# Cross-attention with LayerNorm on one core: the residual and LayerNorm passes of six late tiles moved to PSUM, GpSimd's gain and shift passes separated, and every engine's order of work replaced

## The chip, the cores and the metric

The kernel runs on one core of one Trainium2 chip. The metric is the device time of one execution in microseconds (us). Five engines work at the same time, each through its own queue in program order: TensorE (PE, with its weight loads PEld), VectorE (DVE), ScalarE (ACT), GpSimd (POOL) and SyncE (SP), which only issues DMAs here. An engine waits for another one by a semaphore. SBUF is the on-chip memory, and PSUM holds the results of matmuls in eight banks of 128 x 512 float32.

## The reference

Four batches of 2048 rows attend to 77 context rows each, with 16 heads of width 32. The keys past a batch's length are masked out. The residual is the query itself, and a LayerNorm with gain and shift closes the layer.

```python
qs = (q @ wq).reshape(Bq, Lq, H, HD).transpose(0, 2, 1, 3)
ks_ = (k @ wk).reshape(Bq, Lk, H, HD).transpose(0, 2, 1, 3)
vs = (v @ wv).reshape(Bq, Lk, H, HD).transpose(0, 2, 1, 3)
scores = jnp.einsum('bhqd,bhkd->bhqk', qs, ks_) / jnp.sqrt(jnp.float32(HD))
scores = jnp.where(mask[:, None, :, :], -jnp.inf, scores)
attn_w = jax.nn.softmax(scores, axis=-1)
attn = jnp.einsum('bhqk,bhkd->bhqd', attn_w, vs)
attn = attn.transpose(0, 2, 1, 3).reshape(Bq, Lq, H * HD)
out = attn @ wo + q
mu = jnp.mean(out, axis=-1, keepdims=True)
var = jnp.mean((out - mu) ** 2, axis=-1, keepdims=True)
return (out - mu) / jnp.sqrt(var + EPS) * gamma + beta
```

x has shape (4, 2048, 512), the context (4, 77, 512), and every weight is 512 x 512, all float32.

## The kernel before

The 8192 rows are cut into 64 tiles of 128 rows, into 32 blocks of two tiles, and into 16 groups of four tiles. Products that must keep float32 accuracy are made from a high and a low part of each operand (names ending in h and l): three matmuls for each of four chunks of 128 input columns, so twelve matmuls of 128x512 for a projection. A tile passes through these steps; the letter is the word for the step in the list `ORDER`, and the lines are those of the profile of the kernel before.

- **Q, q** (L274, L288): TensorE projects the queries of a group into a PSUM bank, VectorE copies them out. The split operands come from **i** (ScalarE, L264) and **j** (GpSimd, L268).
- **S** (L398): the scores of a tile, 32 small matmuls into four banks, one for each head of a group of four.
- **T** (L415): VectorE adds the mask, finds the negative row maximum `nm` of a head, and moves the scores into one of three buffers `pbuf`.
- **e** (L430): ScalarE takes the exponentials in place, with the row sums.
- **r, n** (L440, L445): reciprocals on VectorE, then GpSimd multiplies a whole tile by them. For tile 63 these stand in halves (**h, m**, L451, L457).
- **t** (L466): VectorE transposes 32x32 blocks into `B`. **P** and **U** (L477) are the DMAs that regroup `B` into `PT`, twelve for a block, or for one of the tiles 62 and 63; the last letter of the word is the queue (s: SP, a: ACT, g: GpSimd).
- **V** (L491), or **W** for one tile (L506): the product with the values, into two banks. **a, b** or **c, d** (L520, L524): ScalarE rounds the result to its high part `AH`, VectorE forms the low part `AL` and so frees the bank.
- **x** (L532) loads the residual rows. **O** (L547): the output projection, twelve matmuls into a bank. **+** (L556): VectorE adds the residual, writes the sum into SBUF and frees the bank.
- **s** (L567, L568): mean and variance. For the tiles 0 to 55, **v** (L573 to L576) makes the scale and bias of two tiles on GpSimd, **k** (L582) applies them on ScalarE, and **f** (L586, L587) multiplies by `gam` and adds `bet` on GpSimd, two passes one behind the other.
- The tiles 56 to 63 go another way: **s** (L595, L597), **u** (L601, L602) on GpSimd for the inverse deviation, **y** (L613) on VectorE, which subtracts the mean and multiplies by `gam`, and **z** (L616) on VectorE, which multiplies by the inverse deviation and adds `bet`. For 62 and 63, **X** (L536) adds the residual on TensorE, so that no + is needed, and y reads PSUM. The rows of 56 to 59 lie in a buffer that the trace calls `xth`, those of 60 to 63 in `xtl`.
- **w** (L590): SP stores the tile.

Nothing is scheduled by a planner at build time. `ORDER` lists all words once, and the program is recorded in that order, so the sequence of an engine's own words in the list is the sequence of its queue. `SLOTS` says beside it which of an operand's buffers, or which PSUM bank ("mm"), each new tile takes. A word whose buffer still has a reader waits for that reader. The numbers behind a word are tile, block or group and a part: `T61.2` is the third quarter of the maxima of tile 61.

Of the kernel before, what the change touches and what calls it, by code (L numbers as in the profile page):

```python
# [13 lines left out]
ALU = mybir.AluOpType  # L14
# [40 lines left out]
M16.4 e7.1 T7.3 r6 T7.0 P1.8s P1.5s P1.11s P1.9s P1.1s e7.3 e5.1 P1.10s j6 x3 T5.2 q11 e5.2 T5.3 Q10 q10 Q13 q13 T7.2
e7.2 e7.0 Q12 n6 t6 e5.3 r7 n7 S9 T9.2 e9.2 q12 r5 n5 T9.3 Z1.s V0 Y0 Z3.s g9 g8 T9.0 t7 P3.7s P3.5s P3.2s P3.4s V1
a1.0 b1.0 i9 P3.3s P3.10s T9.1 a0.1 b0.1 a1.1 a0.0 t5 P2.0s Q14 b1.1 Z10.s P3.1s P2.6s S8 T8.3 e9.1 e9.3 P3.9s P3.0s
b0.0 T8.1 P3.8s O2 T8.0 i8 j8 j9 +2 s2 O3 T8.2 +3 e8.3 s3 S10 T10.1 v1 e9.0 r9 n9 P3.11s e8.0 M20.4 P3.6s P2.7s g10
T10.2 T10.0 e8.2 e8.1 r8 n8 e10.0 P2.1s O0 +0 q14 s0 t9 Z5.s k3 P2.11s Q15 T10.3 P2.9s f3 t8 k2 f2 e10.2 S11 T11.0
# [5 lines left out]
P5.5s S15 x5 P5.1s T15.3 T15.2 V4 P5.4s a4.0 b4.0 e14.3 T15.0 j11 e14.1 a4.1 e15.2 s4 b4.1 +5 r14 s5 v2 e15.3 e15.0
n14 Q17 Z4.s O9 P5.2s P5.9s P5.0s x8 P5.11s +9 T15.1 q17 P5.10s e15.1 k5 O8 +8 P6.4s S16 T16.0 T16.3 T16.2 e16.2 V5
a5.0 k4 P6.7s P6.2s t14 P6.6s P6.10s P6.0s P6.9s S17 T17.0 g12 P6.3s T17.3 T16.1 e16.1 e17.3 r15 b5.0 Q20 f0 s8 w0
P6.8s x12 P6.5s T17.1 s9 T17.2 a5.1 e16.3 b5.1 f5 n15 t15 v4 f4 P6.1s w5 P6.11s Q21 Q22 S18 T18.2 T18.1 e16.0 r16 g13
P7.6s e17.0 n16 k9 P7.9s P7.4s q20 q21 P7.2s T18.3 T18.0 e17.2 e17.1 r17 n17 P7.8s P7.11s x10 O11 V6 a6.0 b6.0 t16
P7.10s w4 S19 T19.0 +11 s11 t17 k8 f8 a6.1 i12 e18.0 i13 P7.7s f9 O10 w7 P7.0s P7.1s j13 T19.3 b6.1 e18.3 e18.2 T19.1  # L70
q22 Q23 q23 k6 e19.0 e18.1 T19.2 e19.2 r18 O12 +12 S20 T20.1 e20.1 T20.2 e20.2 P8.7s j12 +10 s10 P8.2s P7.5s P7.3s O13
x13 +13 s13 T20.3 P8.0s T20.0 n18 t18 P8.3s g15 P8.10s e19.1 i15 e19.3 r19 Q25 q25 f6 v5 k11 S21 T21.2 P8.5s w9 P8.8s
P8.11s V7 P8.1s a7.0 b7.0 w8 T21.3 x14 P8.6s e20.3 Q24 T21.0 a7.1 b7.1 n19 s12 j15 t19 T21.1 e21.3 e20.0 r20 P8.4s
e21.2 w6 g14 P8.9s x15 P9.5s P9.4s S22 T22.1 T22.0 T22.3 T22.2 M24.4 P9.9s x17 O14 O15 +15 x16 e21.0 k10 e21.1 r21
P9.6s P9.3s v6 f11 i14 +14 n20 t20 V8 a8.1 a8.0 b8.0 n21 t21 S23 T23.1 T23.3 k12 f12 f10 j14 e22.3 b8.1 s14 q24 e22.1
e23.1 T23.2 e23.3 Q27 q27 Q26 P9.1s P9.0s q26 T23.0 s15 e23.2 e22.2 P9.2s P9.7s g16 P10.0s O16 +16 P10.1s P9.11s P9.8s
P9.10s O17 e22.0 r22 +17 P10.10s S24 T24.0 T24.3 T24.2 P10.4s P10.2s P10.6s T24.1 w11 i16 e23.0 k13 r23 w10 n22 t22
e24.3 V9 a9.0 P10.7s P10.8s x19 S25 b9.0 T25.1 s16 v7 e24.0 g17 x18 L2 a9.1 b9.1 P10.5s T25.2 T25.3 k15 w12 P10.11s
j16 P10.3s P10.9s n23 f13 w13 s17 v8 T25.0 Q28 t23 P11.5s P11.6s g18 Q29 e25.1 e24.2 e24.1 r24 n24 q28 O18 +18 S26
P11.2s T26.1 T26.0 P11.11s x20 P11.10s q29 T26.2 T26.3 s18 i17 e25.3 k17 e25.0 f17 e25.2 r25 w17 P11.8s O19 +19 s19  # L80
P11.1s t24 M32.4 P11.4s P11.0s n25 P11.7s t25 V10 S27 T27.1 T27.3 e26.2 k14 e26.0 a10.1 e26.3 a10.0 b10.0 e26.1 f15
r26 P12.7s b10.1 j17 v9 T27.0 Q30 q30 k16 e27.3 P12.5s Q31 q31 T27.2 x21 P12.1s P11.9s O21 P11.3s P12.8s x23 S28 T28.0
T28.2 T28.1 +21 e27.0 k19 O20 n26 t26 s21 e27.1 e27.2 i18 V11 a11.0 b11.0 M44.4 e28.2 S29 T28.3 a11.1 r27 b11.1 O22
O23 T29.2 T29.1 +20 s20 P12.6s T29.0 w15 f14 f19 f16 n27 e28.1 t27 P12.9s S30 T29.3 T30.2 P12.3s P12.0s P12.11s g19
e28.3 e28.0 P12.2s r28 M40.4 x22 w19 +22 +23 Q35 q35 P12.4s i19 j19 Q32 e29.0 T30.0 T30.1 e29.1 e29.2 e29.3 r29 x24
P12.10s P13.4s P13.11s P13.9s P13.5s P13.8s P13.1s P13.6s w14 w16 g20 n28 t28 v10 P13.3s k20 s23 S31 T31.0 n29 s22
T30.3 V12 e30.1 a12.0 k18 e30.0 f18 j18 v11 T31.3 e31.3 t29 e30.2 a12.1 P13.0s P13.7s e30.3 x25 w18 P14.3s P13.2s
P13.10s T31.1 e31.0 e31.1 b12.0 P14.5s P14.7s T31.2 f20 b12.1 Q34 q34 Q33 e31.2 r30 n30 q32 k23 i20 O25 x27 g21 x26
P14.9s +25 q33 s25 P14.1s O24 +24 r31 n31 f23 P14.4s P14.6s S32 T32.3 T32.2 e32.3 e32.2 P14.0s P14.2s P14.8s P14.11s
P14.10s V13 a13.0 S33 a13.1 T32.0 e32.0 t30 s24 v12 T33.0 T33.3 e33.3 Q38 t31 P15.10s j20 T32.1 e32.1 e33.0 T33.1  # L90
e33.1 b13.0 q38 r32 n32 k24 f24 Q37 P15.5s P15.1s k21 P15.8s f21 b13.1 T33.2 Q36 q36 i21 k25 S34 T34.1 T34.0 T34.2 g23
T34.3 t32 V14 a14.1 P15.0s P15.4s P15.3s P15.11s b14.1 a14.0 M36.4 P15.9s e33.2 r33 n33 O26 b14.0 +26 S35 T35.3 T35.2
P15.7s w23 w21 P15.6s w20 x29 e34.3 j21 e34.2 k22 f22 T35.1 e34.1 e34.0 t33 P15.2s Q39 P16.10s P16.0s P16.1s P16.2s
i23 q39 T35.0 O27 q37 +27 g22 s26 s27 v13 w22 P16.4s L3 O29 +29 e35.3 r34 S36 T36.2 T36.1 T36.0 e35.2 e35.0 P16.7s x28
P16.3s P16.11s e36.1 e35.1 x32 T36.3 P16.6s n34 t34 S37 T37.3 r35 T37.1 P16.8s T37.2 e36.2 Q42 f25 Q41 q41 V15 q42 S38
n35 P16.9s t35 P16.5s P17.4s j23 P17.5s P17.1s T38.0 P17.0s i22 j22 k27 x30 P17.11s T38.2 f27 e36.3 e36.0 T37.0 r36
# [76 lines left out]
def xattn_layernorm(  # L173
# [384 lines left out]
    def hold(t):  # L558
        nc.scalar.copy(once(tmps, t // 2, [P, 2, D], F32, "xtf")[:, t % 2], pos.pop(t))
# [199 lines left out]
```

## Time and profile before

| what | us |
|---|---|
| median of 3 runs | 522.41 (521.73 to 524.83) |
| the profiled execution, its own time | 522.61 |
| its span, first to last instruction | 520.8 |
| busy in that span: DVE | 473.8 |
| busy in that span: ACT | 465.6 |
| busy in that span: POOL | 427.3 |

The profile is one execution. "Busy" is the time in which an engine has at least one instruction under way; matmuls overlap by design, so a busy TensorE may still have short pauses between groups. The view by windows gives busy times for stretches of the span. The chain of waits follows the work that ended last back from the end: each step goes to what released it. The word "issue" there means that the engine waited for nothing that the profile shows. The granted clock is the share of TensorE's full clock.

### The profile page before, as it was taken

Reading aid. Unit: us, or ns where it says so; the run is one execution under the profiler, and the core shown is the slowest. Engines: PE = TensorE matmul, PEld = TensorE weight load, DVE = VectorE, ACT = ScalarE, POOL = GpSimd, SP = SyncE. Lnnn points to the kernel's source line nnn. Section 1 sums busy time; section 2 is a strip of 40 time slices with the busy share of each in tenths; the row PEclk is TensorE's granted clock in tenths of the full one; section 3 lists DMA queues with packets and bytes.
Section 4 is the critical chain, followed back from the end, with each engine's and each line's share of the span. In section 5 each row is a group of like instructions: output and inputs, shape, how many; then the busy total and the mean of one; then the engine's idle time right before and its main releaser. Section 6 shows DMA issues by size and latency. Waiting matters only on the chain.

```text
span 520.8 us, 20280 instructions
## 1 busy us (share of the span) xinstructions
PE 502.8 (97%) x6833; PEld 385.6 (74%) x6833; DVE 473.8 (91%) x2562; ACT 465.6 (89%) x2223; POOL 427.3 (82%) x387
## 2 busy tenths in 40 slices
PE   8999999999999999999999999999999999989983
PEld 6987767777777677777778777777777777767752
DVE  5798989999988999999899899999998999879997
ACT  6699999899899999999999999999999999979430
POOL 2574737857888889988988989989888998978896
PEclk9999999999999999999999999999999999989998
DMA  8946776877768786779878679967768777876635
GB/s 302 402 132 206 176 212 180 236 185 187 195 183 260 210 227 213 216 219 240 202 214 228 176 226 276 230 178 200 203 183 256 224 204 199 251 218 161 184 98 222
DMA packets 59261, 110.85 MB, mean 213 GB/s; under 512 B 9430, under 2 KB 11758, under 8 KB 59158
## 3 DMA queue, kind: packets, MB, share of 16 engines
q1 hardware_dynamic: 55702, 102.75, 69.4%
q0 software_dynamic: 2496, 5.77, 4.0%
q8 instruction: 54, 0.88, 0.8%
q10 hardware_dynamic: 960, 1.05, 0.7%
q14 instruction: 49, 0.40, 0.3%
HBM read 41.79 MB, written 16.78 MB: 112 GB/s over the span
## 4 chain that ended last, share of the span: by engine, by line
PE 69%; DVE 13%; DMA 6%; POOL 5%; SPq 3%; issue 2%; ACT 1%; ACTq 0%; DVEq 0%; POOLq 0%
PE po L547 25%; PE pq L274 25%; PE pa L491 9%; PE sc L398 8%; DVE pbuf L415 2%; DVE B L466 2%; SPq L477 2%; DMA PT<-B 2%; PE pk L297 1%; POOL pbuf L445 1%; POOL o L587 1%; POOL o L586 1%; DMA xtf<-xT 1%; DVE st L595 1%; ACT pbuf L430 1%
## 5 line engine op out<-in xcount | busy, mean ns | idle before, releaser
L430 ACT ACTIVATE pbuf<-pbuf,nm 128x77 f32<-128x77 f32 x1024 | 352.7, 353 | 8.7 <-DVE nm L415 8.4
L430 ACT ACTIVATION_READ_ACCUMULATOR pbuf<-pbuf,nm 128x1 f32 x1024 | 198.0, 193 | 0.0
L445 POOL TENSOR_TENSOR pbuf<-pbuf,ri 128x1232 f32<-128x1232 f32 x63 | 142.7, 2269 | 43.4 <-DVE ri L440 33.5
L415 DVE CUSTOM_DVE_ANT_0 pbuf<-sc,mb 128x77 f32<-128x77 f32 x1024 | 171.1, 231 | 6.5 <-PE sc L398 4.1
L547 PE MATMUL po<-woh,AH 128*128 128x512 f32 x256 | 104.1, 407 | 0.2 <-PE sc L398 0.2
L547 PE MATMUL po<-woh,AL 128*128 128x512 f32 x256 | 100.8, 394 | 3.0 <-DVE AL L524 3.0
L274 PE MATMUL pq<-xth,wqh 128*128 128x512 f32 (+1 forms) x256 | 100.8, 394 | 1.0 <-DVE nm L415 0.5
L547 PE MATMUL po<-wol,AH 128*128 128x512 f32 x256 | 100.5, 392 | 0.0
L466 DVE STREAM_TRANSPOSE B<-pbuf 128x1280 f32<-128x1280 f32 x64 | 95.8, 1500 | 3.0 <-POOL pbuf L445 1.3
L274 PE MATMUL pq<-xtl,wqh 128*128 128x512 f32 (+1 forms) x256 | 98.2, 383 | 0.0
L274 PE MATMUL pq<-xth,wql 128*128 128x512 f32 (+1 forms) x256 | 98.1, 383 | 0.0
L415 DVE DVE_READ_ACCUMULATOR2_ANT nm<- 128x1 f32 x1024 | 84.2, 82 | 0.0
L587 POOL TENSOR_TENSOR o<-o,bet 128x512 f32<-128x512 f32 x56 | 73.2, 1307 | 4.4
L586 POOL TENSOR_TENSOR o<-o,gam 128x512 f32<-128x512 f32 x56 | 73.1, 1305 | 3.3 <-ACT o L582 3.3
L268 POOL TENSOR_TENSOR xtl<-xtf,xth 128x1024 fp32r<-128x1024 f32 x28 | 67.6, 2418 | 7.8 <-ACT xth L264 7.8
L398 PEld LDWEIGHTS sc<-kct,q 32*64 32x64 f32 x4096 | 51.9, 130 | 24.8 <-issue 17.7
L398 PE MATMUL sc<-kct,q 32*64 32x77 f32 x4096 | 61.6, 238 | 3.0 <-issue 2.3
L491 PE MATMUL pa<-PT,vsb 96*32 96x256 f32 x992 | 59.7, 382 | 0.9 <-DMA vsb<-v 0.9
L547 PEld LDWEIGHTS po<-woh,AL 128*128 128x128 f32 x256 | 48.4, 189 | 15.0 <-DVE AL L524 4.7
L274 PEld LDWEIGHTS pq<-xth,wqh 128*128 128x128 f32 x256 | 48.0, 188 | 15.2 <-issue 2.5
L547 PEld LDWEIGHTS po<-woh,AH 128*128 128x128 f32 x256 | 48.3, 189 | 13.8 <-issue 1.6
L547 PEld LDWEIGHTS po<-wol,AH 128*128 128x128 f32 x256 | 48.5, 190 | 9.8 <-issue 0.5
(99 smaller groups left out, 647.0 us busy)
## 6 DMA issues: line engine op xcount, KB each, us to landing
PT<-B SPq DMA_DIRECT2D x343, 128.0 KB, 3.4
xtf<-xT SPq DMA_DIRECT2D x28, 512.0 KB, 5.0
o<-x SPq DMA_DIRECT2D x56, 256.0 KB, 5.3
out<-o SPq DMA_DIRECT2D x56, 256.0 KB, 4.2
PT<-B POOLq DMA_DIRECT2D x25, 128.0 KB, 4.4
xtf<-xT SPq DMA_DIRECT2D x4, 256.0 KB
stage_a<-wq SPq DMA_DIRECT2D x4, 256.0 KB, 5.0
stage_a<-wk SPq DMA_DIRECT2D x4, 256.0 KB
```

The source lines that it names most:

```text
L268: nc.gpsimd.tensor_tensor(l[:, c : c + 2], fx.pop((g, c)), xh[g][:, c : c + 2].bitcast(F32), ALU.subtract)
L274: nc.tensor.matmul(pq, w[:, c, m * P : (m + 1) * P], r[g][:, c, rs], start=(n == 0), stop=(n == 11))
L398: mm = nc.tensor.matmul(sc[j][r0 : r0 + SR, g * NK : (g + 1) * NK], qs[q, g, rs.start + r0 : rs.start + r0 + SR], kct[q, g, t // TPB, keys ...
L415: nc.vector.tensor_tensor_reduce(pb[:, h // 2, (h % 2) * NK : (h % 2 + 1) * NK], scs[t][j][:, g * NK : (g + 1) * NK], mb[:, t % TPB, keys_ ...
L430: nc.scalar.activation(pb[:, h // 2, (h % 2) * NK : (h % 2 + 1) * NK], pb[:, h // 2, (h % 2) * NK : (h % 2 + 1) * NK], AF.Exp, bias=nmax[t ...
L445: nc.gpsimd.tensor_tensor(pv, pv, rv.to_broadcast((P, NP, 2, NK)), ALU.mult)
L466: nc.vector.transpose(bt.rearrange("p c q r -> p q c r"), pbuf[t % NPB].rearrange("p q (c r) -> p q c r", c=5),)
L477: parts.setdefault(b, []).append(queue.dma_start(pt[32 * c : 32 * c + 32, i, :, cols], src))
L491: nc.tensor.matmul(pas[b, g // 2][HD * j : HD * (j + 1), (g % 2) * BLK : (g % 2 + 1) * BLK], vsb[:, 2 * b // TPB, h % 2, HD * (h // 2) : H ...
L547: nc.tensor.matmul(pos[t], a[:, c, rs], w[:, c, :], start=(first and c == 0 and n == 0), stop=(c == NC_D - 1 and n == 2),)
L586: nc.gpsimd.tensor_tensor(o, o, gam, ALU.mult)
L587: nc.gpsimd.tensor_tensor(o, o, bet, ALU.add)
```

## The change

The diff does three things.

1. A new word `&` (`residual_psum`) takes the place of `+` for the tiles 56 to 61. It adds the residual in place in the PSUM bank. The statistics of these tiles then read PSUM, `centre` works in place in PSUM, and `finish` reads PSUM and writes the SBUF tile that is stored. The bank is free only after `finish`. For 62 and 63 the residual stays on TensorE, and `centre` now leaves its result in PSUM too.
2. `affine` (word `f`) is split into `gain` (word `f`, the multiplication by `gam`) and `shift` (a new word `)`, the addition of `bet`), so that other GpSimd work can stand between the two passes of a tile.
3. `ORDER` and `SLOTS` are replaced. Apart from the six `&` and the 56 `)`, the new list has the same words as the old one, DMA queues included.

```diff
+    def residual_psum(t):
+        nc.vector.tensor_tensor(pos[t], pos[t], od[t], ALU.add)
+
...
-    def affine(t):
-        o = od[t]
-        nc.gpsimd.tensor_tensor(o, o, gam, ALU.mult)
-        nc.gpsimd.tensor_tensor(o, o, bet, ALU.add)
+    def gain(t):
+        nc.gpsimd.tensor_tensor(od[t], od[t], gam, ALU.mult)
+
+    def shift(t):
+        nc.gpsimd.tensor_tensor(od[t], od[t], bet, ALU.add)
...
     def centre(t):
-        nc.vector.scalar_tensor_tensor(od[t], pos.pop(t, od[t]), mvs[t, 1][:, 0:1], gam, ALU.subtract, ALU.mult)
+        v = pos.get(t, od[t])
+        nc.vector.scalar_tensor_tensor(v, v, mvs[t, 1][:, 0:1], gam, ALU.subtract, ALU.mult)
 
     def finish(t):
-        nc.vector.scalar_tensor_tensor(od[t], od[t], mvs[t, 1][:, 2:3], bet, ALU.mult, ALU.add)
+        nc.vector.scalar_tensor_tensor(od[t], pos.pop(t, od[t]), mvs[t, 1][:, 2:3], bet, ALU.mult, ALU.add)
...
-62.3a U62.0a U62.4a W62 U63.1a y59 u58 v27 k55 k47 f53 U63.2s U63.11s W63 w53 y58 z57 w57 k54 f54 w54 +60 s60 z56 u60
...
+b30.0 U63.8g f53 y56 z56 a30.1 b30.1 U62.11a U63.2s U63.10g U63.1a f55 f52 s58 u58 y59 X62 O61 &61 z59 s61 u61 z57 O60
...
-    "o": "765401234567321706507316240576143206751234601720315642073612534",
+    "o": "765401234567143650247153064261370562140765231407523460745216025",
```

The lists below are the rows of an engine's queue, each with its line, its operation, what it writes and what it reads; the first number in a name is the tile or block, and the last one, or the only one, is a running number. The lines of the new kernel lie a few numbers higher: L557 is `+`, L560 is `&`, L619 `centre`, L622 `finish`, L589 `gain`, L592 `shift`.

**VectorE in the last microseconds.** This is the stretch around the low parts of block 30 (AL_30), before:

```order
L524 TENSOR_TENSOR AL_30_8914<-pa_30_0_8890,AH_30_8908 128x512
L613 SCALAR_TENSOR_TENSOR xth_14_7678<-xth_14_7678,mvt_57_8872,gam_76 128x512
L524 TENSOR_TENSOR AL_30_8914<-pa_30_1_8891,AH_30_8908 128x512
L613 SCALAR_TENSOR_TENSOR xth_14_7678<-xth_14_7678,mvt_59_8886,gam_76 128x512
L613 SCALAR_TENSOR_TENSOR xth_14_7678<-xth_14_7678,mvt_58_8912,gam_76 128x512
L616 SCALAR_TENSOR_TENSOR xth_14_7678<-xth_14_7678,mvt_57_8872,bet_77 128x512
L556 TENSOR_TENSOR xtl_15_7768<-po_60_8921,xtl_15_7768 128x512
L595 BN_STATS st_60_9009<-xtl_15_7768 128x6
L597 BN_AGGR mvt_60_9011<-st_60_9009 128x2
L616 SCALAR_TENSOR_TENSOR xth_14_7678<-xth_14_7678,mvt_56_8804,bet_77 128x512
```

And the same stretch in the new kernel:

```order
L525 TENSOR_TENSOR AL_30_8917<-pa_30_0_8896,AH_30_8914 128x512
L619 SCALAR_TENSOR_TENSOR po_56_8834<-po_56_8834,mvt_56_8857,gam_76 128x512
L622 SCALAR_TENSOR_TENSOR xth_14_7670<-po_56_8834,mvt_56_8857,bet_77 128x512
L525 TENSOR_TENSOR AL_30_8917<-pa_30_1_8897,AH_30_8914 128x512
L600 BN_STATS st_58_8931<-po_58_8874 128x6
L602 BN_AGGR mvt_58_8933<-st_58_8931 128x2
L619 SCALAR_TENSOR_TENSOR po_59_8861<-po_59_8861,mvt_59_8891,gam_76 128x512
L560 TENSOR_TENSOR po_61_8940<-po_61_8940,xtl_15_7695 128x512
L622 SCALAR_TENSOR_TENSOR xth_14_7670<-po_59_8861,mvt_59_8891,bet_77 128x512
L600 BN_STATS st_61_8955<-po_61_8940 128x6
```

The residuals, statistics, centrings and finishes now have a PSUM operand (`po`) where they had only SBUF ones (`xth`, `xtl`), and the finish of tile 56 stands ahead of the second low part of block 30 instead of behind the statistics of tile 60.

**TensorE around the scores of the tiles 60 and 61.** Before, the product of block 27 stands between the two (x8: eight such rows in a row):

```order
L398 MATMUL sc_60_1_8259<-kct_74,q_15_8049 64x77
L398 MATMUL sc_60_2_8260<-kct_74,q_15_8049 64x77
L398 MATMUL sc_60_3_8261<-kct_74,q_15_8049 64x77
L491 MATMUL pa_27_0_8308<-PT_27_7975,vsb_75 32x256 x8
L491 MATMUL pa_27_1_8309<-PT_27_7975,vsb_75 32x256 x8
L398 MATMUL sc_61_0_8350<-kct_74,q_15_8049 64x77
```

In the new kernel the output projection of tile 50 follows the scores of tile 60:

```order
L399 MATMUL sc_60_1_8268<-kct_74,q_15_7997 64x77
L399 MATMUL sc_60_2_8269<-kct_74,q_15_7997 64x77
L399 MATMUL sc_60_3_8270<-kct_74,q_15_7997 64x77
L548 MATMUL po_50_8339<-woh_72,AH_25_7960 128x512
L548 MATMUL po_50_8339<-wol_73,AH_25_7960 128x512
L548 MATMUL po_50_8339<-woh_72,AL_25_7982 128x512
```

The twelve matmuls of that projection now lie between the scores of 60 and 61, and the product of block 27 comes after the scores of 61.

**GpSimd between the normalisations of the tiles 62 and 63.** Before:

```order
L445 TENSOR_TENSOR pbuf2_82<-pbuf2_82,ri_62_8699 128x8x154
L477 DMA PT_30_8664<-B_30_8584 32x2x512
L586 TENSOR_TENSOR o_51_8068<-o_51_8068,gam_76 128x512
L587 TENSOR_TENSOR o_51_8068<-o_51_8068,bet_77 128x512
L573 TENSOR_TENSOR rn_26_8770<-mv_26_8729,small_78 128x2
L574 TENSOR_TENSOR rn_26_8770<-rn_26_8770,small_78 128x2
L575 TENSOR_TENSOR rn_26_8770<-mv_26_8729,rn_26_8770 128x2
L576 TENSOR_TENSOR rn_26_8770<-rn_26_8770,small_78 128x2
L477 DMA PT_31_8757<-B_31_8755 32x2x256
L457 TENSOR_TENSOR pbuf0_80<-pbuf0_80,ri_63_8792 128x4x154 x2
```

And in the new kernel:

```order
L446 TENSOR_TENSOR pbuf2_82<-pbuf2_82,ri_62_8681 128x8x154
L589 TENSOR_TENSOR o_51_8068<-o_51_8068,gam_76 128x512
L592 TENSOR_TENSOR o_50_7588<-o_50_7588,bet_77 128x512
L592 TENSOR_TENSOR o_51_8068<-o_51_8068,bet_77 128x512
L458 TENSOR_TENSOR pbuf0_80<-pbuf0_80,ri_63_8782 128x4x154 x2
```

The four small steps of block 26 and a DMA have moved behind the normalisation of tile 63, and the shift of tile 50, now apart from its gain, stands in their place.

More of the change, by code (lines that the diff above doesn't have):

```diff
@@ L55 @@
[L55 to L59, printed above, removed]
@@ L65 @@
[L65 to L69, printed above, removed]
@@ L70 @@
[L70 to L94, printed above, removed]
@@ L154 @@
     "xtl": "10101010101010101",
[L155 to L156 removed]
+    "xtf": "010101100110101001100101010110",
+    "PT": "10100101010101010101010101010101010",
     "B": "0101011010101010101010101010101010",
```

165 lines of the change are left out of this document (99 added, 66 removed).

## The prediction

> **What bounds the kernel now.** I read the page's busy times first, then the windows, to see where TensorE is not busy, then the chain of waits at those places.
>
> ```profile
> PE 502.8 (97%) x6833; PEld 385.6 (74%) x6833; DVE 473.8 (91%) x2562; ACT 465.6 (89%) x2223; POOL 427.3 (82%) x387
> ...
> core 0: us, PE busy (x) PEld busy (x) DVE busy (x) ACT busy (x) POOL busy (x), PEclk, DMA share, GB/s
> 0.00:52.00 52.00, 49.96 (x632) 41.64 (x633) 40.24 (x215) 42.37 (x183) 25.77 (x27) 1.00 0.77 261
> 52.00:416.00 364.00, 360.77 (x5060) 276.16 (x5059) 339.76 (x1934) 351.86 (x1700) 310.73 (x257) 1.00 0.77 212
> 416.00:442.00 26.00, 26.00 (x431) 18.94 (x429) 25.34 (x169) 26.00 (x141) 23.86 (x24) 1.00 0.72 204
> 442.00:468.00 26.00, 23.91 (x364) 18.65 (x360) 20.85 (x115) 22.11 (x112) 22.29 (x25) 0.93 0.84 233
> 468.00:494.00 26.00, 26.00 (x248) 19.04 (x233) 24.56 (x100) 18.67 (x88) 22.92 (x29) 1.00 0.67 176
> 494.00:507.00 13.00, 11.08 (x118) 7.65 (x111) 12.83 (x20) 4.57 (x7) 12.36 (x18) 1.00 0.35 108
> 507.00:521.00 14.00, 5.12 (x22) 3.55 (x20) 10.25 (x16) 0.00 (x0) 9.39 (x13) 0.82 0.53 206
> ```
>
> TensorE carries the kernel: from 52 to 416 us it lacks 364.00 - 360.77 = 3.2 us. A new order with the same matmuls can give back those 3.2 us, 2.1 us between 442 and 468, and what the end costs. In the last 27 us it is no longer TensorE: from 494 to 507 VectorE is busy 12.83 of 13 us, and it runs on after TensorE is done. So the time is a TensorE stream of some 490 us and a VectorE tail.
>
> The one large pause in the stream, in the chain of waits:
>
> ```profile
> 454.00 0.88 PE sc L398 x52
> 454.88 1.86 PE pa L491 x32
> 456.75 0.81 PE sc L398 x49
> 457.56 2.08 issue
> 459.65 0.36 PE sc L398 x6
> 460.01 7.31 PE po L547 x24
> ...
> 468.20 5.64 PE po L547 x24
> ```
>
> TensorE stops for 2.08 us within the scores of tile 61, for nothing that the profile shows as a wait. The two projections behind it (24 matmuls) then take 7.31 us, where the next two take 5.64: 1.67 us more. The windows there give the clock, and the DMA view of 456 to 459 us a packet:
>
> ```profile
> 460.00:465.00 5.00, 5.00 (x17) 3.94 (x16) 2.93 (x27) 1.91 (x9) 3.90 (x5) 0.66 0.56 161
> 465.00:468.00 3.00, 3.00 (x75) 2.31 (x73) 1.97 (x12) 3.00 (x19) 1.43 (x1) 1.00 0.92 269
> ...
> q8 instruction: 54, 0.88, 0.8%
> ...
> q8 instruction: 1, 0.02, 2.5%
> ```
>
> The granted clock was 0.66 in the 5 us behind the pause, and 1.00 later. The whole run has 54 packets on the instruction queue q8 (first q8 row), one of them in just these 3 us (second). TensorE has 2 x 6833 = 13,666 records, 253 for each packet. From the scores of tile 60 to those of 61 it goes through 128 + 64 + 128 = 320 records in 3.6 us (454.00 to 457.56), more than a packet's worth. I read the pause as instructions that came too late.
>
> **The change part by part.**
>
> *The PSUM passes.* No instruction is added on VectorE; operands change. What they cost now:
>
> ```profile
> L616 DVE SCALAR_TENSOR_TENSOR xth<-xth,mvt,bet x4: 747/1266/1760, 499.5 to 504.1; 128x512 f32<-128x512 f32 x4
> L616 DVE SCALAR_TENSOR_TENSOR xtl<-xtl,mvt,bet x4: 721/752/1444, 510.9 to 516.9; 128x512 f32<-128x512 f32 x4
> ...
> L613 DVE SCALAR_TENSOR_TENSOR xth<-xth,mvt,gam x4: 718/743/746, 493.4 to 498.9; 128x512 f32<-128x512 f32 x4
> L613 DVE SCALAR_TENSOR_TENSOR xtl<-xtl,mvt,gam x2: 749/1198/1647, 507.9 to 511.6; 128x512 f32<-128x512 f32 x2
> L613 DVE SCALAR_TENSOR_TENSOR xtl<-po,mvt,gam x2: 719/729/739, 513.9 to 516.1; 128x512 f32<-128x512 f32 x2
> ```
>
> The undisturbed time is about 0.75 us. Where they took longer, GpSimd was in its own 128x512 passes:
>
> ```profile
> 501.75 4.14 DVE L616 SCALAR_TENSOR_TENSOR xth<-xth,mvt,bet 128x512 f32<-128x512 f32 x3
> ...
> 502.05 1.60 POOL L587 TENSOR_TENSOR o<-o,bet 128x512 f32<-128x512 f32 x1
> 503.61 1.72 POOL L586 TENSOR_TENSOR o<-o,gam 128x512 f32<-128x512 f32 x1
> 505.41 1.60 POOL L587 TENSOR_TENSOR o<-o,bet 128x512 f32<-128x512 f32 x1
> ...
> 512.96 1.34 POOL L586 TENSOR_TENSOR o<-o,gam 128x512 f32<-128x512 f32 x1
> 513.92 0.72 DVE L613 SCALAR_TENSOR_TENSOR xtl<-po,mvt,gam 128x512 f32<-128x512 f32 x1
> ```
>
> The last two rows are the test inside this trace: the centring of tile 62 reads PSUM, ran beside a gain pass, and took 0.72 us. So the disturbance belongs to the form with two SBUF tensors, and the change removes that form from all fourteen late passes that have it (six centrings, eight finishes). The excess: two finishes at 1.76 instead of 0.75 (2.0), one at 1.44 (0.7), one centring at 1.65 (0.9), in sum 3.6 us. They lie on VectorE's gapless tail, so I take -3.6; it could be nothing if the tail is then set by GpSimd or by TensorE.
>
> Writing PSUM from VectorE (six residuals, eight centrings) has no row. The nearest are these, which read PSUM:
>
> ```profile
> L556 DVE TENSOR_TENSOR xth<-po,xth 128x512 f32<-128x512 f32 x4 | 2.6, 662 | 0.0
> L595 DVE BATCH_NORM_STATS2 st<-xtl 128x6 f32<-128x512 f32 x2 | 1.4, 696 | 0.1
> L595 DVE BATCH_NORM_STATS2 st<-po 128x6 f32<-128x512 f32 x2 | 1.4, 687 | 0.0
> ```
>
> I take no difference. Bounds: 14 passes between the shortest and the longest undisturbed row of this size, 0.66 and 0.75, so -1.3 to +1.3 us.
>
> [...]
>
> *Banks held longer.* A bank of 56 to 61 is free only after its finish. The new table gives the bank of 56 to the projection of tile 60, and that of 59 to the product of tile 63. Both finishes stand on VectorE ahead of work that TensorE needs anyway (the second low part of block 30; the low parts of 62), so the cover is VectorE's own order: 0. If it is gone, a late bank costs a finish or two, up to 1.5 us.
>
> *The split of gain and shift.* Two passes as before, so no extra work; one takes 1.31 us in the mean:
>
> ```profile
> L587 POOL TENSOR_TENSOR o<-o,bet 128x512 f32<-128x512 f32 x56 | 73.2, 1307 | 4.4
> ```
>
> Behind the normalisation of tile 63, GpSimd had 10 such passes and has 8 now: 2.6 us earlier there, off the path. But the last inverse deviation, for tile 63, now stands behind a shift (of tile 52); if that runs late, the end waits up to 1.3 us. I take 0, since GpSimd starts that stretch with less to do.
>
> *The order around the scores of 61.* The projection of tile 50 (2.8 us, half of the 5.64) now stands between the scores of 60 and 61. The 320 records get 2.8 us more, which is over the 2.08 us that were missing. I take the pause as gone, -2.1, and with it the slow clock, -1.7. Bounds: 0 if it comes back here or elsewhere.
>
> *The rest of the order.* The matmuls are the same 6833, and the changes from one kind of group to another on TensorE are 171 in both lists. So the stream keeps its length, and what can change is the 3.2 us of pauses between 52 and 416. The place with the least room is ScalarE: 351.86 of 364 us busy. The new list draws the scores of the tiles 13 to 28 ahead by about two groups of twelve matmuls (5.6 us), which gives ScalarE and VectorE less time to clear the banks. I leave 3.2 as it is, with bounds of 0 and 6.4, so -3.2 to +3.2. Moved DMAs:
>
> ```profile
> o<-x SPq DMA_DIRECT2D x56, 256.0 KB, 5.3
> ```
>
> On SP, the loads of the residual rows 52 and 59 are moved behind regroupings of the blocks 29 and 30. A load lands 5.3 us after its issue; the residuals that read them stand behind the transposition of tile 62 and in the last 27 us, so I cost it at 0. If that cover is gone, VectorE waits, and all of its tail with it.
>
> **The sum.** -3.6 - 2.1 - 1.7 = -7.4 us on a profiled execution of 522.61 (span 520.8): 515.2. The median of the runs, 522.41, is 0.2 lower, so 515.0.
>
> **The rivals.**
>
> 1. *The pause comes back*, at 60 and 61 or at another place where scores follow each other closely. For it: the cause is only read from one packet's place, and there are about as many such places in the new list (12, with at most one product or a pair of products between two scores, against 11). Then only the tail is gained: 522.4 - 3.6 = 518.8. [...]
> 2. *The tail does not shorten.* With VectorE faster, the last inverse deviations on GpSimd (12.36 of 13 us busy from 494 to 507) set the end, or the late banks do: +1.3 and +1.5 and the PSUM writes +1.3 eat the 3.6, and the time is 522.4 - 7.4 + 4.1 = 519.1, or 522.9 with the pause back as well.
> 3. *Slower: instructions late at several places.* Each such pause costs 2.08 + 1.67 = 3.75 us, since TensorE has no reserve. Against the -7.4, two are a draw, and from three on the kernel is slower: 515.0 + 3 x 3.75 = 526.3, with four 530.0. For it: the same DMA load. Against it: 11 places before gave one large pause.
>
> **How the numbers follow.** A measurement of this kernel can tell about 1% (5.2 us) from no change, so faster means under 517.2 and slower over 527.6. The forecast, 515.0 with 511.5 to 517.2 by the bounds of the other pauses, has 0.50. Rival 1 has 0.26 and rival 2 0.14, both within 1%. Rival 3 has 0.10, of which 0.03 stays within 1% and 0.07 goes beyond. So faster 0.50, same 0.43, slower 0.07. The range goes from 515.0 - 3.2, rounded down to 511.5, to 522.5, near the end of rival 2, and leaves out rival 3 and about 0.1 at its edges.
>
> **What the new profile would show.** Right: centrings and finishes of the late tiles between 0.70 and 0.80 us even beside GpSimd's passes; the passes of GpSimd in the last 25 us at 1.3; no pause of over 1 us within scores, and the granted clock at 1.00 from 440 to 500; the last finish about 7 us earlier. Wrong: a busy share of TensorE between 52 and 416 that falls by several us; "issue" with over 1 us in its chain; idle time of VectorE in the tail that ends on the inverse deviations or on an x load; residuals into PSUM well over 0.75 us.

## The result, and the profile after

| | median, us | runs | ratio to the kernel before, 95% interval |
|---|---|---|---|
| kernel before | 523.13 | 14 | |
| new kernel | 519.32 (516.80 to 522.49) | 14 | 0.9933 (0.9906 to 0.996) |
| new kernel, second set, beside runs of before at 522.80 | 521.08 (516.58 to 523.99) | 12 | 0.9964 (0.9933 to 0.9996) |

The change makes the kernel about 0.5% faster: 3.8 us in the first set, 1.7 in the second. The 26 runs of both sets have a median of 519.94. That is within 1%, where 1.4% faster was forecast. The profiled execution took 516.82 us (span 514.8), one of the fastest.

The view by windows of the new kernel, in the columns of before:

```profile
52.00:416.00 364.00, 361.74 (x5152) 276.71 (x5151) 338.76 (x1955) 354.80 (x1721) 312.60 (x257) 1.00 0.76 210
442.00:468.00 26.00, 24.00 (x387) 17.67 (x369) 24.84 (x142) 23.99 (x122) 22.39 (x25) 1.00 0.86 224
...
494.00:507.00 13.00, 13.00 (x111) 10.08 (x111) 12.47 (x23) 1.17 (x2) 12.65 (x17) 1.00 0.54 190
```

TensorE is now busy for all of the 13 us from 494 to 507 (11.08 before), so the pauses that it had in this stretch are gone. From 442 to 468 it lacks 2.00 us, as before (2.09), though the slow clock there is gone (1.00 for 0.93).

The passes of the tail, grouped (last columns: busy time, mean ns of one, idle time ahead):

```profile
L619 DVE SCALAR_TENSOR_TENSOR po<-po,mvt,gam 128x512 f32<-128x512 f32 x8 | 5.9, 745 | 0.0
L600 DVE BATCH_NORM_STATS2 st<-po 128x6 f32<-128x512 f32 x8 | 5.5, 688 | 0.0
L622 DVE SCALAR_TENSOR_TENSOR xtl<-po,mvt,bet 128x512 f32<-128x512 f32 x4 | 3.0, 742 | 0.2
L622 DVE SCALAR_TENSOR_TENSOR xth<-po,mvt,bet 128x512 f32<-128x512 f32 x4 | 2.9, 733 | 0.1
L560 DVE TENSOR_TENSOR po<-po,xth 128x512 f32<-128x512 f32 x4 | 2.7, 676 | 0.0
```

And the timeline where GpSimd has a pass of its own under way:

```profile
506.05 1.30 POOL L592 TENSOR_TENSOR o<-o,bet 128x512 f32<-128x512 f32 x1
...
506.49 0.72 DVE L622 SCALAR_TENSOR_TENSOR xth<-po,mvt,bet 128x512 f32<-128x512 f32 x1
507.12 0.74 DVE L622 SCALAR_TENSOR_TENSOR xtl<-po,mvt,bet 128x512 f32<-128x512 f32 x1
```

No centring or finish is stretched any more, and neither are GpSimd's passes (1.60 to 1.72 us before). The chain of waits shows where the two microseconds from 442 to 468 went:

```profile
450.47 3.10 DVE mb L382
453.58 0.61 DVE q L289
454.19 0.04 issue
454.23 0.82 PE sc L399 x44
455.05 2.96 PE po L548 x12
458.01 0.88 PE sc L399 x52
458.89 0.99 PE pa L492 x13
459.88 1.02 issue
460.89 1.49 PE pa L492 x19
```

VectorE's mask operation (`mb`, word M, tiles 60 to 63) takes 3.10 us, a copy of a query projection waits behind it, and the scores of tile 60 stop for 0.98 us until that copy is done. GpSimd issues two DMAs from 449.96 us on and normalises a tile from 451.08 to 453.35; the mask operation ends 0.22 us behind that. And a pause without a wait ("issue", 1.02 us) stands in the product of block 27.

One table serves all that follows. For each profile it has the time between the starts of three scores on TensorE, and from the last of them to the end of the span. The work in each stretch is the same in both orders.

| profile | 58 to 60 | 60 to 62 | 62 to end |
|---|---|---|---|
| before | 22.25 | 13.32 | 53.54 |
| new, first profile | 22.45 | 12.39 | 49.56 |
| new, second profile | 24.33 | 10.79 | 49.59 |
| new order without PSUM operands | 24.34 | 10.77 | 53.68 |
| PSUM operands in the old order | 22.34 | 13.33 | 50.82 |
| new, mask early | 23.39 | 9.63 | 49.63 |
| new, mask early, regroupings first | 22.64 | 9.56 | 49.55 |
| old order, projection moved | 22.40 | 9.81 | 54.25 |
| old order, projection moved, PSUM operands | 22.25 | 9.77 | 51.41 |

### The profile page after: what moved, and what is told of

It is laid out like the page before. It is cut to its first block, busy times and chain, and to the rows that moved or that the text cites. A ratio compares the mean times of both kernels' runs of the same rounds, so it can differ in the third digit from the quotient of the medians.

```text
span 514.8 us, 20308 instructions
## 1 busy us (share of the span) xinstructions
PE 501.3 (97%) x6833; PEld 383.9 (75%) x6833; DVE 471.5 (92%) x2562; ACT 465.6 (90%) x2223; POOL 421.6 (82%) x387
## 3 DMA queue, kind: packets, MB, share of 16 engines
q10 hardware_dynamic: 960, 1.05, 0.8%
## 4 chain that ended last, share of the span: by engine, by line
PE 58%; DVE 18%; DMA 8%; POOL 6%; ACT 3%; SPq 3%; issue 3%; DVEq 0%; POOLq 0%; ACTq 0%
PE po L548 25%; PE pq L275 19%; PE pa L492 7%; PE sc L399 7%; DVE pbuf L416 5%; DVE B L467 5%; DMA PT<-B 4%; POOL pbuf L446 3%; ACT pbuf L431 2%; DMA stage_a<-xT 2%; DVE AL L525 1%; DVE q L289 1%; SPq L478 1%; DMA o<-x 1%; DMA stage_a<-wk 1%
## 5 line engine op out<-in xcount | busy, mean ns | idle before, releaser
L589 POOL TENSOR_TENSOR o<-o,gam 128x512 f32<-128x512 f32 x56 | 72.2, 1293 | 2.9 <-ACT o L586 2.4
L592 POOL TENSOR_TENSOR o<-o,bet 128x512 f32<-128x512 f32 x56 | 72.1, 1291 | 1.5
L275 PEld LDWEIGHTS pq<-xth,wql 128*128 128x128 f32 x256 | 48.1, 188 | 9.6
```

The costliest lines, as they stand in the source:

```text
L275: nc.tensor.matmul(pq, w[:, c, m * P : (m + 1) * P], r[g][:, c, rs], start=(n == 0), stop=(n == 11))
L589: nc.gpsimd.tensor_tensor(od[t], od[t], gam, ALU.mult)
L592: nc.gpsimd.tensor_tensor(od[t], od[t], bet, ALU.add)
```

## The experiments

**The new kernel once more.** No edit.

> The new kernel once more, nothing edited, for a second profile and as the ground for the others of this set. The first profile of it (span 514.8 us) has two pauses of TensorE behind 452 us: 0.98 us within the scores of tile 60, which end on VectorE's copy of a query projection, and 1.02 us within the product of block 27 that nothing in the trace explains (read as late instructions). Theory A (the first is a wait that the new order brings, the second is chance): the first stands there again with 0.9 to 1.2 us; the second is gone, elsewhere, or longer and followed by a granted clock well below 1.00, and that is why 14 runs of this kernel spread from 516.8 to 522.5. Theory B (both belong to the order): both are there again within 0.2 us, and the spread comes from something else. Time: 519.3 us by either, as in the 14 runs.

521.08 us. The first pause stands there again (1.21 us from one matmul to the next, as in the first profile), the second does not: theory A. But a wait that the first profile hardly had (0.40 us) is now large. Ahead of the transposition of tile 54, VectorE is idle (timeline), and later the mask operation comes as before (chain):

```profile
431.39 1.51 DVE L467 STREAM_TRANSPOSE B<-pbuf 128x1280 f32<-128x1280 f32 x1 [2.27 <-POOL o L592]
```

The row names a shift on GpSimd, which had ended 0.45 us before; the next experiments show that it is the regroupings of block 25 that the transposition waits for.

```profile
455.57 3.09 DVE mb L382
458.66 0.61 DVE q L289
```

**The mask early.** One word moved on VectorE.

```diff
-T55.3 M56.4 e54.3
+T55.3 M56.4 M60.4 e54.3
...
-q62 P28.9s M60.4 Q61
+q62 P28.9s Q61
```

> The new kernel with the mask of the tiles 60 to 63 made right behind that of 56 to 59 (near 417 us) instead of near 450 us, where VectorE's one mask operation took 3.10 us (0.36 us at 417 us) while GpSimd was in a normalisation, and the copies of the query projections stood behind it. Theory A (that operation holds up the scores of tile 60): no pause over 0.3 us within the scores of 60, the operation at 0.33 to 0.40 us, and the time 1.0 to 1.5 us below the new kernel's, about 518.1. Theory B (VectorE is late there anyway, or TensorE loses the same time at the next wait): within 0.4 us of the new kernel's time.

518.63 us (516.00 to 520.32, 6 runs), ratio 0.9913 (0.9879 to 0.9947). The operation takes 0.38 us there, the scores of 60 run through, and the time is 1.3 us below the 519.94 of the 26 runs (2.5 below the 521.08 of the same set): theory A. The wait ahead of the transposition is left:

```profile
431.18 1.51 DVE L467 STREAM_TRANSPOSE B<-pbuf 128x1280 f32<-128x1280 f32 x1 [1.33 <-DMA PT<-B]
```

**The new order without the PSUM operands.**

```diff
-&57 s53 ... O56 &56 ... O61 &61
++57 s53 ... O56 +56 ... O61 +61
...
-        v = pos.get(t, od[t])
-        nc.vector.scalar_tensor_tensor(v, v, mvs[t, 1][:, 0:1], gam, ALU.subtract, ALU.mult)
+        nc.vector.scalar_tensor_tensor(od[t], pos.pop(t, od[t]), mvs[t, 1][:, 0:1], gam, ALU.subtract, ALU.mult)
...
-        nc.vector.scalar_tensor_tensor(od[t], pos.pop(t, od[t]), mvs[t, 1][:, 2:3], bet, ALU.mult, ALU.add)
+        nc.vector.scalar_tensor_tensor(od[t], od[t], mvs[t, 1][:, 2:3], bet, ALU.mult, ALU.add)
```

> The new order and the split of gain and shift, but the residuals, centrings and finishes of the late tiles in SBUF as before. Theory A (the PSUM operands carry the gain, by keeping VectorE's passes out of GpSimd's way): 3.6 us slower than the new kernel, so 522.9 us, no different from the kernel before; finishes or centrings of over 1.2 us beside GpSimd's passes of 128x512. Theory B (the order makes the gain): 519.3 us as the new kernel, with the passes at 0.75 us because GpSimd's work stands elsewhere now.

523.55 us, ratio 1.0013 (0.9987 to 1.0039): nothing is left of the gain, theory A. Without them the new order is 2.5 us slower than the 521.08 of the same set and 3.6 slower than the 26 runs. By the table, the stretch from 60 to 62 is 2.6 us shorter than before, that from 58 to 60 is 2.1 longer, and the tail is as long as before. In its timeline both sides are stretched again:

```profile
508.69 1.27 POOL L589 TENSOR_TENSOR o<-o,gam 128x512 f32<-128x512 f32 x1
...
509.05 1.45 DVE L621 SCALAR_TENSOR_TENSOR xth<-xth,mvt,bet 128x512 f32<-128x512 f32 x1
510.04 1.59 POOL L592 TENSOR_TENSOR o<-o,bet 128x512 f32<-128x512 f32 x1
510.43 1.75 DVE L621 SCALAR_TENSOR_TENSOR xtl<-xtl,mvt,bet 128x512 f32<-128x512 f32 x1
```

**The PSUM operands in the old order.** The same functions as in the new kernel, `&` for `+` at 56 to 61, and other banks for the last five accumulators:

```diff
-...3142560317256"
+...3142560370321"
```

> The kernel before, in its own order, with the PSUM operands alone: residuals of 56 to 61 in place in PSUM, centrings in PSUM, finishes from PSUM; the last five accumulators get other banks, since a bank is now held until its finish. Gain and shift stay together. Theory A: every centring and finish at 0.70 to 0.80 us, the tail from the scores of tile 62 to the end 3.6 us shorter, and the time 523.1 - 3.6 = 519.5 us. Theory B (the tail is then set by GpSimd's inverse deviations, which stand behind two passes in a row): less than half of that, over 521.3 us.

519.77 us, ratio 0.9939 (0.9918 to 0.996): 3.0 us, theory A, with 2.7 of the 3.6 in the tail. And its chain repeats the pause of before at the very same place:

```profile
456.33 0.82 PE sc L398 x48
457.15 2.12 issue
459.27 0.36 PE sc L398 x6
459.64 7.28 PE po L547 x24
```

**Loads moved away from 412 to 455 us**, with the mask early.

```diff
-S62
+S62 x63 x57
...
-S63
+S63 x58 x62 x61 x60
```

> The new kernel with the early mask (518.6 us before this edit), and six loads of residual rows (tiles 57, 58, 60, 61, 62, 63; 256 KB each), which the order issues between 412 and 455 us, moved behind the scores of the tiles 62 and 63. Two of three profiles of the new order show VectorE idle for 2.27 us ahead of the transposition of tile 56, until regroupings of an earlier block have landed, while the DMA engines are 0.82 busy there; TensorE then loses 1.4 us at the scores of 58 and 0.6 behind. Theory A (the crowd of loads makes the landings late): that wait falls below 0.6 us, the DMA share of 416 to 442 falls by about 0.08, and the time by 1.5 to 2 us to about 517. Theory B (the regroupings queue behind one another, the loads don't matter): 518.6 us, the wait as before.

520.41 us (518.17 to 526.48), ratio 0.9956 (0.9921 to 0.9992). Neither theory: the wait ahead of the transposition (it is that of tile 54, not 56) is still 1.76 us, since these loads stand behind the regroupings in question, and a new one has come. On SP's queue, six loads now stand ahead of the last regrouping of block 29:

```profile
467.72 0.60 SPq L533 DMA_DIRECT2D xtl<-x  x1
468.37 0.99 SPq L533 DMA_DIRECT2D xth<-x  x2
469.40 2.52 SPq L533 DMA_DIRECT2D xtl<-x  x3
471.96 0.60 SPq L478 DMA_DIRECT2D PT<-B  x1
```

The product of block 29 then starts 2.14 us late, and the clock is slow behind it (0.59 from 479 to 483 us). That pointed to the order on the queue, rather than to the sum of the traffic.

**Gain and shift joined.** Each `)` right behind its `f`, in the new order.

```diff
-f55 f52 ... )55 w55 )53 w53
+f55 )55 f52 )52 ... w55 w53
```

> The new kernel with each shift put right behind its gain again, as one step, all else as it is. Theory A (the split is worth nothing, as the prediction took it): the time of the new kernel (median of its 26 runs so far about 520), and 49.6 us from the scores of tile 62 to the end, as in both profiles of it. Theory B (the split lets the inverse deviations go ahead of shifts and brings the last 1.3 us of the tail, which is 4.0 us shorter with order and split and 2.7 with the PSUM operands alone): about 521.3, with 50.9 us from the scores of 62 to the end.

527.63 us, ratio 1.0079 (1.0047 to 1.0111): both theories are too small. In this order 7.7 us hang on the split. In the tail, the finish of tile 61 waits for its inverse deviation, which stands behind three whole steps of GpSimd:

```profile
510.58 0.75 DVE L622 SCALAR_TENSOR_TENSOR xtl<-po,mvt,bet 128x512 f32<-128x512 f32 x1 [2.76 <-POOL mvt L607]
```

The rest is lost ahead of the tail: from 52 to 484 us VectorE's transpositions wait 8.9 us for GpSimd's normalisations, and 3.6 in the second profile of the new kernel. What the split would bring in the old order was not tried.

**The projection between.** The old order with the PSUM operands, and one word moved (with its bank).

```diff
-S61 T61.2 f49 e60.2 e60.1 T61.0 e60.3 T61.3 O50
+O50 S61 T61.2 f49 e60.2 e60.1 T61.0 e60.3 T61.3
```

> The kernel before with the PSUM operands (519.8 us), and in its order one word moved: the projection of tile 50 from behind the scores of 61 to ahead of them, so that 12 wide matmuls stand between the product of block 27 and the scores of 61. Its profile had a pause of 2.12 us after 56 of the 64 scores of tile 61 and a slow clock behind it, as the kernel before. Theory A (instructions come too late there, since three dense groups follow each other): the pause is under 0.5 us, the two projections behind it take 5.7 us instead of 7.3 in sum, and the time is 519.8 - 3.8 = 516.0. Theory B (a hidden wait or a slow fetch that the move only shifts): the pause is there again, within or behind the scores of 61, and the time is 519.8 within 0.6.

516.86 us (516.07 to 517.43), ratio 0.9873 (0.9831 to 0.9914): theory A, 2.9 us for one word. No pause without a wait of over 0.4 us is left in its profile.

**The stream shifted.** The same PSUM kernel, only the warm-up differs.

```diff
-    for i in range(WARM):
-        nc.tensor.matmul(pw, warm[:, :P], warm, start=True, stop=True)
+    for i in range(WARM + 24):
+        nc.tensor.matmul(pw[:, :64], warm[:, :P], warm[:, :64], start=True, stop=True)
```

> The kernel before with the PSUM operands (519.8 us) and its order untouched. The nine wide matmuls that warm TensorE at the start are replaced by 33 narrow ones, so that every later instruction of TensorE stands 24 matmuls (48 queue entries with their weight loads) further back in the stream. In the kernel before, in the one with PSUM operands and in the first profile of the new one the pause without a wait came behind matmul number 6376 or 6377, counted from the start, though other work stands there in the new order. Theory A (the pause is a block of instructions that arrives late, so it belongs to a number in the stream): behind number 6376 again, which is now after 32 of the 64 scores of tile 61 instead of 56. Theory B (it belongs to the work, by a wait that the trace does not show): after 56 of the scores of 61, as before. Time 519.8 by either.

528.87 us, ratio 1.0101 (1.0067 to 1.0135): 9 us slower, which neither theory had. The pause in the scores of 61 is gone, and four others have come. The largest, in the chain, and the clock behind it:

```profile
379.76 1.86 PE pa L491 x32
381.63 0.78 PE sc L398 x47
382.41 2.82 issue
385.23 0.38 PE sc L398 x11
385.60 6.60 PE pq L274 x21
```

```profile
385.00:389.00 4.00, 3.77 (x20) 2.92 (x20) 3.42 (x22) 4.00 (x23) 2.80 (x3) 0.59 0.70 164
```

So I counted, in the program of each kernel, at which entry of TensorE's queue the matmul behind such a pause stands (pauses of over 0.6 us with no wait; matmuls counted from 0):

| kernel | pause, us | after matmul | entry | entry modulo 256 |
|---|---|---|---|---|
| before; PSUM in the old order | 2.09; 2.13 | 6376 | 12994 | 194 |
| new, first profile | 1.02 | 6377 | 12994 | 194 |
| new, mask early | 0.73 | 979 | 1987 | 195 |
| stream shifted | 0.88 | 1856 | 3779 | 195 |
| stream shifted | 2.09 | 3490 | 7107 | 195 |
| stream shifted | 2.82 | 5249 | 10691 | 195 |
| stream shifted | 0.63 | 5879 | 11971 | 195 |
| low parts moved (below) | 2.11 | 3490 | 7107 | 195 |
| two loads moved (below) | 0.68 | 3490 | 7107 | 195 |
| two loads moved (below) | 1.46 | 6376 | 12994 | 194 |

All lie at the same place of a block of 256 entries, whatever work stands there. The trace of before has 13,941 records of TensorE (13,666 matmuls and weight loads and 275 others) and 54 packets of 16 KB on the instruction queue (0.88 MB), 258 records a packet, so I take one block of 256 entries for one packet, an estimate from these numbers: entry 1987 is 7.8 blocks of 256 into the program and 7 packets had been fetched by then, entry 12994 is 50.8 blocks in and 50 packets had been fetched, and so for every row. In each of them TensorE went on 1.2 to 1.6 us after the last of these packets had landed, and in the profile of before it reached that entry in each of the other blocks no earlier than 1.39 us after the landing. So the late block is the cause. That is theory A in substance; only its guess that the pause must fall at number 6376 again was wrong, since there are 53 such places, and which of them was late differed between the kernels of the table. At most of the 53 borders of a profile TensorE went on without a pause (in the kernel before, one of them had over 0.6 us); at the ones in the table it stopped for up to 2.82 us.

**Regroupings first.** The new kernel, mask early, and two transfers moved on SP.

```diff
-P25.8s P25.5s x50 P25.3g )43 w43 t53 P26.5s ... P25.0s ... P25.6s v22
+P25.8s P25.5s P25.3g )43 t53 P26.5s ... P25.0s ... P25.6s w43 x50 v22
```

> The new kernel with the early mask (518.6 us), with one store (tile 43) and one load (residual rows of tile 50), 256 KB each, moved on SP's queue from ahead of the last two regroupings of block 25 to right behind them. VectorE's transposition of tile 54 waits for those regroupings: idle for 1.33 us ahead of it in the kernel with the early mask, 2.27 and 2.32 in two profiles of the new order, 0.40 in the first. Theory A (transfers of the same queue go in turn, so the wait is the price of what stands ahead of the regroupings): at some 240 GB/s, 512 KB are about 2.1 us, so the wait is gone (below 0.4 us), the holes of TensorE at the scores of 58 and behind (0.48 + 0.63 us) with it, and the time is about 517.5. Theory B (the landings are late because all engines of the DMA are full there, in whatever order): the wait stays over 1 us and the time at 518.6.

516.88 us (512.81 to 518.17, 6 runs), ratio 0.9871 (0.984 to 0.9902): theory A for the wait. The transposition has none, though the DMA is as full as before (window of this kernel, last columns):

```profile
427.37 1.51 DVE L467 STREAM_TRANSPOSE B<-pbuf 128x1280 f32<-128x1280 f32 x1
```

```profile
420.00:428.00 8.00, 7.95 (x156) 6.49 (x155) 7.46 (x48) 8.00 (x42) 7.89 (x8) 1.00 0.96 268
```

The 240 GB/s of the expectation were the author's estimate; in the second profile of the new kernel the DMA moved 224 GB/s from 416 to 442 us, and 284 from 420 to 428.

The time is less sure. The medians, each of six runs, lie 1.7 us apart, but the intervals of the two ratios overlap. In the profiles the stretch from 58 to 60 is 0.75 us shorter; the profile with the early mask had, besides, a hole of 2.05 us on TensorE at 256 us, at a place that this edit does not touch.

**The projection moved in the kernel before**, SBUF operands and all.

```diff
-S61 ... T61.3 O50
+O50 S61 ... T61.3
```

> The kernel before, with its own SBUF operands, and the projection of tile 50 ahead of the scores of 61 instead of behind them; nothing else. Theory A (the pause of 2.1 us and the slow clock behind it are worth what the prediction took, and are gone with this one move): 522.8 - 3.6 = 519.2 us, no pause without a wait over 0.5 us, and 53.5 us from the scores of 62 to the end as before. Theory B (the tail takes the gain back, since VectorE with its stretched passes sets the end): over 521.5.

519.93 us, ratio 0.9926 (0.9893 to 0.996): 3.1 us, theory A. Its chain, in place of the one that the prediction quotes:

```profile
457.29 2.97 PE po L547 x12
460.26 0.88 PE sc L398 x52
461.14 2.92 PE po L547 x12
464.06 0.88 PE sc L398 x52
```

**Low parts moved**, on the kernel with the projection between.

```diff
-&59 s59 u59 V30 a30.0 s58 b30.0 X62 y57 a30.1 b30.1
+&59 V30 a30.0 b30.0 s59 u59 a30.1 b30.1 s58 X62 y57
```

> The PSUM operands and the moved projection in the order before (516.9 us), with the two low parts of block 30 on VectorE put ahead of the statistics of tiles 59 and 58, and the second also ahead of the centring of 57. TensorE's projection of tile 60 waits there for the bank that the first low part frees: 1.43 us of pause, 2.56 us more than the matmuls in all. Theory A (that wait carries through to the end): 1 to 1.5 us less, 515.5 to 516. Theory B (VectorE has no gap from there on, so it sets the end and TensorE's gain is idle time): it had 0.80 us of idle time ahead of the first low part of tile 62 and nothing else over 0.3; so at most 0.8 less, 516.1 to 516.9.

518.56 us (516.12 to 522.46): no gain, so theory A is out, and the time lies above the range of theory B too. The profiled run, the slowest, has a pause of 2.11 us at matmul 3490, where its parent's profile has 0.30 with the same work ahead of it:

```profile
256.00 0.73 PE sc L398 x43
256.73 2.11 issue
258.84 0.48 PE sc L398 x18
```

So a place can be late in one execution and not in another, which is part of the spread between runs.

**Two loads moved away from the pause**, in the old order with PSUM operands.

```diff
-P28.0s x60 x52 ... t58 x61 ... S62
+P28.0s x52 ... t58 ... S62 x60 x61
```

> The kernel before with the PSUM operands (519.8 us), its order untouched but for two loads of residual rows (tiles 60 and 61, 256 KB each) that SP issues at 450 and 454 us, moved behind the scores of tile 62. In that profile the DMA engines are 0.99 busy from 452 to 455 us and 1.09 from 455 to 457, and there the block of instructions is fetched (a packet from 456.7 to 458.0 us) whose lateness makes the pause of 2.1 us within the scores of 61. Theory A (the block is late because it stands behind other transfers): with about a third of the bytes gone from 452 to 457 us the pause is under 1 us and the slow clock behind it gone; 2.5 to 3.8 us less, 516 to 517.3. Theory B (the fetch simply starts too late for three dense groups in a row, however free the DMA is): the pause is at the same matmul (number 6376), 1.8 to 2.3 us long, and the time is 519.8 within 0.7.

518.51 us (516.79 to 520.07, 6 runs). Between the theories: same matmul, 1.46 us instead of 2.12, and the slow clock as before (7.26 us for the two projections). Other transfers moved up, so the DMA was still 1.05 busy from 455 to 457 us (1.09 before). How much of the lateness is the DMA's and how much the density of the code stays open.

## Why the prediction was right and wrong

*The PSUM passes, -3.6: right.* Alone they bring 3.0 us, and taken out of the new kernel they cost 2.5 to 3.6. The cause is the one named, the form with two SBUF tensors beside a pass of GpSimd: in the kernel before and in the same kernel with the projection moved, all eight centrings and finishes of over 1 us (1.44 to 1.76 us in the kernel before) ended 0.55 us after a pass of GpSimd had ended.

*Writing PSUM, -1.3 to +1.3: right, at 0.* Centrings take 745 ns (718 to 749 undisturbed before), finishes 733 and 742, residuals into PSUM 676 (656 to 680 into SBUF before), and statistics 688 from PSUM (682 and 696 from SBUF before).

*Banks held longer, 0: right.* TensorE is busy for the whole of 494 to 507 in both profiles of the new kernel.

*The split, 0: too small.* The tail became 4.0 us shorter with order and split, 2.7 with the PSUM operands alone, and joined again it is 4.3 longer. It let the inverse deviations pass ahead of shifts. The prediction looked only at the one deviation that a shift might hold up. What of the 1.3 us (4.0 less 2.7) is the split's, and what the order's, stays open.

*The pause and the slow clock, -3.8: right as a mechanism, too large by 0.7 to 0.9.* The one move that the prediction named brings 3.1 and 2.9 us in the two kernels where it was tried, and 13.3 us between the scores of 60 and 62 become 9.8. That it was a late block of instructions, read there from one packet's place, is shown by the table of entries. "Gone" was too much for the new order: in its first profile the same entry was late again, by 1.02 us, within other work and with no slow clock behind it; in the second it was not.

*The rest of the order, 0: this is the step that failed.* The prediction says "what can change is the 3.2 us of pauses between 52 and 416", and of the moved DMAs "I cost it at 0". The 3.2 held: 2.3 and 4.1 us in the two profiles of the new kernel. But the order brings new waits behind 416 us, where nothing was priced. The old order with the PSUM operands and the moved projection, so with the two gains of the sum alone, takes 516.86 us; the new order, which has the PSUM operands and a projection between those scores as well, takes 519.94. So the rest of the order costs about 3.1 us. The two gains themselves came to 5.9 us (522.71 to 516.86) instead of 7.4.

Two experiments found waits that make up this cost. The mask operation is worth 1.3 us by the medians (519.94 to 518.63) and 1.2 by the stretch from 60 to 62 (10.79 to 9.63). One store and one load ahead of the regroupings are worth 1.7 by the medians (to 516.88) and 0.75 by the stretch from 58 to 60. A third wait, ahead of 416 us, was not edited: the scores of tile 12 wait for regroupings, 0.76 us in the first profile of the new kernel and 1.84 in the second, where the 32 matmuls of the product behind them took 2.83 us (1.86 in the kernel before, at 454.88 us); the kernel before does not wait there. With the measured medians the sum is -3.0 - 3.1 + 1.3 + 1.7 = -3.1, which is about how far 519.94 lies below the kernel before (522.7 to 523.4 in the medians of its sets). That it closes so well is in part luck: it leaves out the third wait and the 1.3 us of the tail named above, and the 1.7 is not clear of the noise.

The mask operation could have been read from the order and the profile of before. That of the tiles 60 to 63 moved from a place at 375 to one at 450 us, ahead of copies that the scores wait for, and the trace of before has its price. The operation by tile (min, median and max ns; first and last start), before and after:

```profile
L381 DVE TENSOR_SCALAR mb<-m x17: 206/358/2192, 16.6 to 375.7; 128x384 bf16<-128x384 uint8 x15, 128x96 bf16<-128x96 uint8 x1, 128x288 bf16<-128x288 uint8 x1
```

```profile
L382 DVE TENSOR_SCALAR mb<-m x17: 208/357/3102, 16.2 to 450.5; 128x384 bf16<-128x384 uint8 x15, 128x96 bf16<-128x96 uint8 x1, 128x288 bf16<-128x288 uint8 x1
```

A longest time of 2192 ns beside a median of 358 says that something shuts the operation out. As to the DMAs, I looked at two moved loads and asked who waits for them; the question was who stands behind them. The window from 420 to 428 us before and after (last columns: DMA share, GB/s):

```profile
420.00:428.00 8.00, 8.00 (x125) 5.93 (x124) 8.00 (x50) 8.00 (x45) 7.82 (x7) 1.00 0.66 193
```

```profile
420.00:428.00 8.00, 7.95 (x156) 6.50 (x155) 6.57 (x32) 8.00 (x49) 7.91 (x8) 1.00 0.99 315
```

*The rivals.* None came out as written. Rival 1, "only the tail is gained", comes nearest to the time (518.8 against 519.3), for another reason: of the pause 1.02 us came back in one of two profiles, and other waits took its place.

Two versions beat both kernels in the median: the old order with PSUM operands and one projection moved (516.86), and the new one with the mask early and the regroupings first (516.88, its best run 512.81).

## What to carry to other kernels

When a whole order is replaced, go through the operations that moved far, the small ones too: for each, ask what is queued behind it on its engine or DMA queue and who waits for that, and look up the longest time that the old trace has for it, not the median. A gain found at one place of a searched order is no gain until the waits that the order brings have been priced as well. For an unexplained pause, count its entry in the queue: here it stayed at 12994 when the work around it changed (2.09 us before, 1.02 in the first profile of the new kernel), which pointed to the instruction stream, and twelve wide matmuls between two dense groups left no pause without a wait of over 0.4 us in the old order.

## What the runs showed of the hardware

VectorE's mask operation (uint8 in, bfloat16 out, SBUF to SBUF) takes 0.36 us alone, and longer beside a pass of GpSimd: in the 14 profiles, all 71 of over 0.6 us (up to 3.10 in the new kernel) ended 0.21 to 0.23 us after such a pass. Beside the same two splits of GpSimd it took 0.70 us in one profile, where it started at 254.27 us, and 2.31 in another, where it started at 254.82 and TensorE stopped for 2.05 us:

```profile
252.24 4.68 POOL L269 TENSOR_TENSOR xtl<-xtf,xth 128x1024 fp32r<-128x1024 f32 x2
...
254.82 2.31 DVE L382 TENSOR_SCALAR mb<-m 128x384 bf16<-128x384 uint8 x1
```

What holds it up there, and whether the centrings and finishes with two SBUF tensors are held up by the same thing, is not shown by any run here.

Moving TensorE's stream by 24 matmuls, with the order unchanged, cost 9 us. In the profiles, some 1.5 of it were lost by the scores of tile 0, behind the shorter warm-up (21.35 to 22.89 us), and 9.4 between these and the scores of 58, where the four pauses and two slow stretches lie. From 60 to 62 it is 4.0 us shorter, and the tail is 2.6 longer, which was not taken apart.

All six pauses without a wait that lasted 1.46 us or more, each within scores, were followed by some 4 us at a lower clock (0.59 in the window above, 0.69 from 459 to 463 us with the PSUM operands in the old order, 0.67 from 460 to 464 in the kernel before). Where wide matmuls follow at once, they took 1.6 to 1.9 us longer in sum. Pauses of that length beside other work were not always followed by it: behind 1.63 us ahead of the second half of a projection, at 506 us in the kernel before, the granted clock stayed at 1.00. What decides is not shown.
